# Moving 16 pieces of the adjacency mask from the first projection into the first attention, and sharing the last scaling between two engines

## The chip, the cores and the metric

The kernel runs on one core of a Trainium2 chip. A core has a matrix engine (TensorE, PE in the profile), a vector engine (VectorE, DVE), an activation engine (ScalarE, ACT), a general engine (GpSimd, POOL) and a queue engine (SyncE, SP). DMA engines move data between the large memory and the on-chip memory; SP, ACT and POOL start transfers. The metric is the device time of one execution in microseconds (us), lower is better.

## The reference, cut to what matters

Four graph layers run one after the other on 3327 nodes with 512 features. Each layer adds its output to its input and normalizes every row (subtract the mean, divide by the root of the variance plus 1e-5). All four use the same 3327 x 3327 integer matrix `adj`. Layers 0, 2 and 3 are graph attention; layer 1 averages up to 64 neighbours. The first layer's attention, cut:

```python
Wh = jnp.einsum('ni,hio->hno', h, W)                    # 8 heads of 64
f1 = jnp.einsum('hno,ho->hn', Wh, a1)
f2 = jnp.einsum('hno,ho->hn', Wh, a2)
e = jax.nn.leaky_relu(f1[:, :, None] + f2[:, None, :], 0.2)
masked = jnp.where(adj[None] > 0, e, NEG_INF)
attention = jax.nn.softmax(masked, axis=-1)
h_prime = jnp.einsum('hnm,hmo->hno', attention, Wh)
```

So every weight of the attention is multiplied by whether `adj` is positive. That mask is needed by all four layers, and it is made once.

## The kernel before, in words

**Tiles and halves.** The 3327 nodes are padded to 3328, which is NT = 26 tiles of 128 rows. The mask lies on chip as one tile `mask` of 128 x 26 x 3328 eight-bit numbers. The nodes that receive (the columns of the transposed matrix `adjT`) are cut into two halves of 1664, and each half into two quarters of 832.

**Making the mask.** A *piece* is one tile of 128 senders by one quarter: `mask_load` (L628) brings 128 x 832 integers of `adjT` into a buffer `raw`, and `mask_set` turns them into zeros and ones, on DVE by a comparison (L639) or on ACT by a steep sigmoid (L638). There are 104 pieces. The list `pieces` (L1103) holds first those of the quarters 0 and 1, tile by tile (52 pieces, the first half of the receivers), then those of quarter 2, then those of quarter 3. `mask_steps` makes a list of steps from them: step k loads piece k and sets piece k minus a lag. A load can start when its buffer is free, that is, when the piece that had it before has been set.

**The first projection (0 to about 142 us).** For each of the 26 tiles `project1` transposes a tile of x on PE (L266) and copies it (L267, ACT); `project2` multiplies it by the weights (16 matmuls L276 into two banks) and DVE empties the banks into `vt` (L282), which POOL's queue stores to memory (L288). One tile's `project2` runs after the next tile's `project1`. In the loop at L1138, after each tile's `project2`, three or four steps are taken alternately from `msteps`, the steps of the first EARLY = 5 x 26 / 2 + 3 = 68 pieces. They use eight buffers and a lag of five; ACT issues the first eight loads, SP the others; all are set by DVE. After tile 14, `prepare` and `cut` work on the columns of half 0, and at tile 20 the first row tiles `rb` are loaded for the attention. At the end `mean` (L298) multiplies a mean row.

**The first attention.** It runs through units (half, s): two halves and, in each, four slots of two heads, in the order (0,0), (0,1), (0,2), (0,3), (1,0) and so on. A unit loops over the 26 sender tiles j. For each j and head DVE makes `t` (L410, the larger of two terms times the mask of the half, 128 x 1664), ACT makes `y` from it (L413), PE multiplies `t` by the values `vj` (L433) and, two j later, `y` by small columns (L385). `t` has six buffers, `y` seven. Two lists are served once for each j: `background` (jobs in the code) and then `aside`. For this attention `aside` holds the steps of the 36 remaining pieces, with two buffers and a lag of one; the list of indices in L1175 says which of them ACT sets (k % 5 in 1, 3), DVE sets the others. They are kept in the program's order. `background` holds the jobs that `first_jobs` (L1155) gives for a unit, followed by those that the unit before left (ten steps of transposing its output and storing it), in this way: in (0,0) two empty jobs, the preparing and cutting for half 1 and eight jobs that count neighbours in half 0; in (0,1) the ten steps and then eight jobs `attend` (a weight load started by ACT, L1116, and eight matmuls, L1122); in (0,2) the ten steps and then eight jobs that count neighbours in half 1, from its mask (`count_jobs`, L669).

**The tail.** After the last layer's attention, `lasts` holds four groups of row tiles (4, 4, 4 and 1). For each group DVE finishes the sums and statistics, ACT takes the root (L1082), and `scale` for the group before it multiplies and shifts each of its tiles, on ACT (L1069) for every fourth tile and on DVE (L1071) for the others. Even tiles are stored by SP's queue, odd ones by POOL's (L133).

**What sets the order.** PE runs in the program's order. For the other engines a scheduler orders the instructions before the run, by its own estimates, unless `keep_in_program_order` pins one. An engine takes its instructions one after the other, so an instruction that waits holds those behind it, and the same holds for the transfers that one engine starts.

Of the kernel before, what the change touches and what calls it, by code (L numbers as in the profile page):

```python
# [32 lines left out]
def kernel(  # L33
# [12 lines left out]
    NT = (N + P - 1) // P  # L46
# [595 lines left out]
    def mask_steps(pool, pieces, lag, on_act, pinned, ahead=0):  # L642
        held = []

        def step(k):
            if k < len(pieces):
                held.append(mask_load(pool, *pieces[k], nc.scalar if k < ahead else nc.sync))
            if k >= lag:
                ins = mask_set(held[k - lag], *pieces[k - lag], on_act=(k - lag) in on_act)
                if pinned:  # L650
                    tc.keep_in_program_order(ins)
                held[k - lag] = None

        return [lambda k=k: step(k) for k in range(len(pieces) + lag)]
# [3 lines left out]
    def count_jobs(pool, half):  # L658
        jobs = []
        for s0, n in QUADS:  # L660
            i0, w_ = (half * HALF + s0) * P, n * P
            held = {}

            def counts(lo, hi, i0=i0, w_=w_, held=held):
                if lo == 0:
                    held["p"] = qp.tile([P, 4 * P], F32, name="pct", tag="q")
                for t in range(lo, hi):
                    g = t % 4
                    nc.tensor.matmul(held["p"][32 * g:32 * g + 32, :w_], onecol[:, 31 - t:63 - t],  # L669
                                     mask[:, t, i0:i0 + w_], start=t < 4, stop=t >= NT - 4)  # L670


            def none(i0=i0, w_=w_, held=held):
                ct = pool.tile([P, 4 * P], BF, name="ct", bufs=1)
                nc.scalar.copy(ct[:, :w_], held["p"][:, :w_])
                pn = qp.tile([P, 4 * P], F32, name="pn", tag="q")
                nc.tensor.matmul(pn[:, :w_], below, ct[:, :w_], start=True, stop=True)
                nc.vector.tensor_scalar(ct[:, :w_], pn[:, :w_], 128.0, None, op0=ALU.min)
                nc.sync.dma_start(out=ctd[:, i0:i0 + w_], in_=ct[:NT + 1, :w_])
                nb = pool.tile([P, 4 * P], F8, name="nb", bufs=1)  # L680
                nc.vector.tensor_scalar(nb[:, :w_], ct[:, :w_], 0.0, None, op0=ALU.is_equal, saturate=False)
                nc.sync.dma_start(out=mask[P - 1:P, NT - 1, i0:i0 + w_], in_=nb[NT:NT + 1, :w_])

            jobs += [lambda f=counts: f(0, NT), none]
        return jobs
# [216 lines left out]
    def third(first):  # L902
        with tc.tile_pool(name="col3", bufs=1) as cp, tc.tile_pool(name="at_r3", bufs=2, reuse_waits="tile") as rp:
# [3 lines left out]
            with tc.tile_pool(name="p_w", bufs=1, reuse_waits="tile") as wp, \  # L907
# [23 lines left out]
                for t0 in range(0, NT, 2):  # L931
# [4 lines left out]
                    for s, y in enumerate(ys):  # L936
                        t = t0 + s
# [22 lines left out]
            with tc.tile_pool(name="f3", bufs=2) as fp, tc.tile_pool(name="f4", bufs=1) as gp:  # L960
# [100 lines left out]
                def scale(q0, n):  # L1061
                    qs = slice(q0, q0 + n)
                    keep(nc.vector.reciprocal(rs[:, qs, 0], rs[:, qs, 0]))
                    keep(nc.vector.scalar_tensor_tensor(rs[:, qs, 1], mv[:, qs, 0], -1.0, rs[:, qs, 0],
                                                        op0=ALU.mult, op1=ALU.mult))
                    for q in range(q0, q0 + n):
                        y = g[:, q, :]
                        if q % 4 == 3:
                            keep(nc.scalar.activation(y, y, AF.Identity, bias=rs[:, q, 1:2], scale=rs[:, q, 0:1]))  # L1069
                        else:  # L1070
                            keep(nc.vector.tensor_scalar(y, y, rs[:, q, 0:1], rs[:, q, 1:2], op0=ALU.mult, op1=ALU.add))  # L1071
                        store(y, HALF + q, q)
# [14 lines left out]
    L0, L2, L3 = Layer(0, 8, False), Layer(2, 8, True), Layer(3, 4, True)  # L1087
# [3 lines left out]
    with tc.tile_pool(name="col0", bufs=1) as cp, tc.tile_pool(name="raw", bufs=2) as rawp, \  # L1091
            tc.tile_pool(name="at_r0", bufs=3, reuse_waits="tile") as rp:
        L0.columns(cp)
        L0.more_columns(cp)
        L0.piece_columns(cp)
        with tc.tile_pool(name="p_w", bufs=1, reuse_waits="tile") as wp, \
                tc.tile_pool(name="p", bufs=3, reuse_waits="tile") as pp, \
                tc.tile_pool(name="p_r", bufs=8, reuse_waits="tile") as rw0, \
                tc.tile_pool(name="p_ps", bufs=2, space=PSUM, reuse_waits="tile") as ps:
            if LAST < P:  # L1100
                nc.gpsimd.memset(mask[:, NT - 1, :], 0.0)
            nc.gpsimd.memset(mask[:, :, N:NP], 0.0)
            pieces = [(t, q) for t in range(NT) for q in range(2)] + [(t, q) for q in (2, 3) for t in range(NT)]  # L1103
            EARLY = 5 * NT // 2 + 3
            msteps = mask_steps(rw0, pieces[:EARLY], 5, (), False, 8)

            def load(t):
                xt = pp.tile([P, F], F32, name="xt", bufs=5)
                load_tile(xt, x, t, nc.sync if t < 3 else nc.gpsimd)
                return xt  # L1110


            def attend(pool, tag, dst, wT, a, k, held):
                H = a.shape[1] // 2
                wt = pool.tile([P, F], F32, name="wt", tag=tag, bufs=FC if tag == "wt" else 1)
                nc.scalar.dma_start(out=wt, in_=wT[k * P:(k + 1) * P, :])  # L1116
                if k == 0:
                    held["a"] = pool.tile([P, FC, 2 * H], F32, name=f"asb{H}", bufs=1)
                    nc.scalar.dma_start(out=held["a"], in_=a.rearrange("(c p) m -> p c m", p=P))
                    held["p"] = qp.tile([P, FC, 2 * H], F32, name="pa", tag="q")  # L1120
                for c in range(FC):
                    nc.tensor.matmul(held["p"][:, c, :], wt[:, c * P:(c + 1) * P], held["a"][:, k, :],  # L1122
                                     start=k == 0 and c == 0, stop=k == FC - 1,
                                     skip_group_check=True)
                if k == FC - 1:
                    nc.vector.tensor_copy(dst, held["p"] if len(dst.shape) == 3 else
                                          held["p"].rearrange("p c (e h) -> p c e h", e=2))

            def bank(e):
                return ps.tile([P, 512], F32, name=f"pw{e}")  # L1130

            xT = L0.project1(pp, ps, load(0), 0)
            held = {}
            wsb = wp.tile([P, FC, 2, FW + L0.H], F32, name="wsb")
            for k in range(FC):
                attend(pp, "wt", wsb[:, :, :, FW:], w0T, a0, k, held)
            load_wide(wsb, w0, nc.scalar)
            pend = (xT, 0)  # L1138
            for t in range(1, NT):
                xT = L0.project1(pp, ps, load(t), t)  # L1140
                L0.project2(pp, bank, wsb, *pend)
                pend = (xT, t)
                for _ in range(3 + t % 2):
                    if msteps:
                        msteps.pop(0)()
                if t == HALF + 1:
                    L0.prepare(pp, 0)
                    L0.cut(pp, 0)
                if t == NT - 6:
                    L0.first_rows = L0.rows(rp, 0, 0)  # L1150
            L0.project2(pp, bank, wsb, *pend)
            for f in msteps:
                f()
            L0.mean(pp, bank, wsb)

        def first_jobs(pool, half, s):

            if (half, s) == (0, 0):
                return [lambda: None] * 2 + [lambda: L0.prepare(f0, 1, "xr", 1, True), lambda: L0.cut(f0, 1, "h", 2, True)] + \
                    count_jobs(pool, 0)  # L1160
            if (half, s) == (0, 2):
                return count_jobs(pool, 1)
            if (half, s) == (0, 1):
                jobs = []
                for li, wT, a in ((2, w2T, a2), (3, w3T, a3)):
                    held = {}
                    jobs += [lambda k=k, li=li, wT=wT, a=a, held=held:
                             attend(f0, "xr", wa[li], wT, a, k, held) for k in range(FC)]
                return jobs
            return []  # L1170


        pieces = pieces[EARLY:]
        ends = []
        L0.attention(rp, first_jobs, mask_steps(rawp, pieces, 1, [k for k in range(len(pieces)) if k % 5 in (1, 3)], True),  # L1175
                     ending=lambda sp: ends.extend(finish(f0, x, L0, 0, 2, 2, nc.sync, None, sp)))

    with tc.tile_pool(name="col2", bufs=1) as cp:
# [60 lines left out]
```

## Time and profile before

| what | value |
|---|---|
| time, median of 3 runs | 3378.35 us (3377.11 to 3380.59) |
| the profiled execution | 3378.99 us, its span 3377.3 us |
| mean granted clock of PE | 0.986 |
| busy: PE, DVE, ACT, POOL | 3252.0, 2687.1, 2358.2, 239.6 us |
| first projection, 0 to 142.26 us: busy PE, DVE, ACT | 122.64, 85.34, 31.04 us |
| moved by DMA in that stretch | 344 GB/s on the average |
| tail, 3340 to 3377.3 us: busy DVE, ACT | 19.84, 13.98 us |

The profile is of one execution. Busy time is the time in which an engine worked; a granted clock of 1.00 is full speed. A row by stretch gives for each engine its busy microseconds and, in brackets, how many instructions began in it. A group's row names the line of the code, the engine, the operation, what it writes and reads, how often, its busy time and mean duration, and after the bar the idle time before it with what ended that time. "A <- B" in a list of waits means that A waited for B. The time of a whole execution is a little longer than its span from the first to the last instruction.

### The profile page before, as it was taken

The numbers are of one execution on the slowest core, as the hardware profiler recorded it, in microseconds if no ns is written. First come the engines' busy times: TensorE is split into PE (matmuls) and PEld (weight loads), VectorE is DVE, ScalarE is ACT, GpSimd is POOL, SyncE is SP. The second block draws the span as 40 slices with busy tenths as digits, with TensorE's granted clock in tenths as the row PEclk, the third lists the DMA queues.
The fourth block names the chain that finished last, engine by engine and source line by source line (L and its number), as shares of the span: only waits on it lengthen the run. The fifth ranks groups of instructions, "written<-read, shape, count | busy, mean of one in ns | idle before, by whom it ended". The sixth has DMA issues, their size and how long they took to land.

```text
span 3377.3 us, 47143 instructions
## 1 busy us (share of the span) xinstructions
PE 3252.0 (96%) x18424; PEld 1627.4 (48%) x18476; DVE 2687.1 (80%) x2619; ACT 2358.2 (70%) x2145; POOL 239.6 (7%) x389
## 2 busy tenths in 40 slices
PE   8799999999989999999989999999998999999997
PEld 7544344444444455545544444444446754455443
DVE  6799999999977544444449999999998766668887
ACT  2398998999953333333338999999997755558985
POOL 3100000000010111111110000000002000010110
PEclk9999999999999999999999999999998999999998
DMA  9544111110143433333320111111117411122311
GB/s 379 212 128 124 49 49 38 55 50 28 45 133 123 143 96 86 89 82 88 81 73 22 45 49 50 51 48 47 35 31 240 156 41 41 43 50 79 96 41 49
DMA packets 288014, 284.29 MB, mean 84 GB/s; under 512 B 107492, under 2 KB 223534, under 8 KB 287791
## 3 DMA queue, kind: packets, MB, share of 16 engines
q1 hardware_dynamic: 254063, 170.62, 16.7%
q0 software_dynamic: 28208, 102.96, 9.5%
q10 hardware_dynamic: 5520, 7.69, 0.7%
q8 instruction: 146, 2.39, 0.3%
q14 instruction: 77, 0.63, 0.1%
HBM read 212.01 MB, written 69.17 MB: 83 GB/s over the span
## 4 chain that ended last, share of the span: by engine, by line
PE 81%; DVE 5%; DMA 5%; issue 5%; ACT 4%; POOL 0%; SPq 0%; POOLq 0%; DVEq 0%; ACTq 0%
PE po L433 49%; PE acc L869 12%; PE pd L385 7%; PE pw L276 4%; DMA raw<-in_adjT_dram 3%; DVE t L410 3%; PE pz L737 3%; PE pi L740 2%; ACT y L413 1%; PE pk L829 1%; PE pt L461 1%; DMA h<-hd 1%; PE pa L1122 0%; DMA dd<-red 0%; PE pct L669 0%
## 5 line engine op out<-in xcount | busy, mean ns | idle before, releaser
L410 DVE SCALAR_TENSOR_TENSOR t<-rb,qc,mask 128x1664 f32<-128x1664 f32 x1040 | 1960.2, 1954 | 169.4 <-PE po L433 147.9
L413 ACT ACTIVATE y<-t,bi,sc 128x1664 fp8e4<-128x1664 f32 x1040 | 1770.5, 1768 | 309.5 <-PE pd L385 292.3
L433 PE MATMUL po<-t,vj 128*64 128x448 f32 (+3 forms) x8320 | 1908.6, 520 | 22.5 <-DVE t L410 19.8
L433 PEld LDWEIGHTS po<-t,vj 128*64 128x64 f32 (+1 forms) x8320 | 838.7, 148 | 970.4 <-issue 702.3
L869 PE MATMUL acc<-zs,kt 128*128 128x512 bf16 x1312 | 393.8, 381 | 2.2 <-issue 0.2
L276 PE MATMUL pw<-wsb,xT 128*128 128x264 f32 (+1 forms) x1248 | 300.2, 395 | 15.3 <-DVE vt L282 13.1
L869 PEld LDWEIGHTS <-kt 128*128 128x128 fp8e4 x2002 | 196.5, 98 | 242.1 <-issue 8.6
L821 ACT CAST pk<-cy 128x512 f32<-128x512 bf16 x169 | 99.1, 588 | 278.2 <-DVE kt L833 267.0
L385 PE MATMUL pd<-y,sden 128*32 128x448 fp8e4 (+1 forms) x4160 | 259.4, 341 | 10.4 <-ACT y L413 10.4
L276 PEld LDWEIGHTS pw<-wsb,xT 128*128 128x128 f32 x1248 | 239.8, 196 | 60.2 <-issue 10.6
L869 PE MATMUL acc<-zl,kt 128*128 128x512 bf16 x638 | 242.4, 380 | 0.6
L385 PEld LDWEIGHTS <-sden 128*32 128x32 bf16 x4160 | 117.5, 96 | 162.6 <-issue 139.8
L833 DVE SCALAR_TENSOR_TENSOR kt<-pk,mask 128x512 fp8e4<-128x512 f32 x169 | 116.1, 688 | 95.8 <-PE pk L829 95.8
L282 DVE TENSOR_TENSOR vt<-pw,dc 128x256 f32<-128x256 f32 x156 | 59.1, 418 | 147.4 <-ACT dc L277 142.7
L364 POOL DMA_DIRECT2D rb<-r x40 | 21.4, 534 | 1668.2 <-DVE t L410 1653.8
L280 ACT COPY rc<-pw 128x8 f32<-128x8 f32 (+1 forms) x78 | 12.7, 163 | 155.6 <-PE pw L276 155.6
L737 PE MATMUL pz<-wn,xT 128*128 128x512 f32 x208 | 95.8, 604 | 1.6 <-ACT xT L731 1.6
L841 DVE SCALAR_TENSOR_TENSOR y<-acc,cnt,bnb 128x512 f32<-128x512 f32 x26 | 19.5, 750 | 96.9 <-PE acc L869 89.5
L705 POOL DMA_DIRECT2D cy<-ctd x91 | 68.1, 748 | 385.5 <-ACT pk L821 312.8
L740 PE MATMUL pi<-wl,xT 128*128 128x512 f32 x208 | 93.5, 592 | 0.0
L639 DVE TENSOR_SCALAR mask<-raw 128x832 fp8e4<-128x832 int32 (+2 forms) x90 | 54.7, 615 | 39.7 <-DMA raw<-in_adjT_dram 39.2
L154 ACT ACT_TABLE_LOAD x46 | 59.0, 1283 | 37.3 <-DVE mv L153 36.7
(187 smaller groups left out, 1704.7 us busy)
## 6 DMA issues: line engine op xcount, KB each, us to landing
vj<-v SPq DMA_DIRECT2D x312, 128.0 KB
rb<-r POOLq DMA_DIRECT2D x40, 832.0 KB, 4.6
raw<-in_adjT_dram SPq DMA_DIRECT2D x67, 416.0 KB
cy<-ctd POOLq DMA_DIRECT2D x78, 256.0 KB, 4.0
h<-hd SPq DMA_DIRECT2D x61, 256.0 KB
v<-vt SPq DMA_DIRECT2D x50, 256.0 KB
hd<-hb SPq DMA_DIRECT2D x48, 256.0 KB
xr<-x POOLq DMA_DIRECT2D x45, 256.0 KB, 3.1
```

The lines of the kernel that those rows point to most:

```text
L276: nc.tensor.matmul(pw[e][:, :FW + H], xT[:, c, :], wsb[:, c, e, :], start=c == 0, stop=c == FC - 1)
L282: nc.vector.tensor_tensor(vt[:, hs, :], pw[e][:, :FW].rearrange("p (h d) -> p h d", d=D), self.dc[:, t, hs].rearrange("p (h e) -> p h e", e=1)
L385: nc.tensor.matmul(pd[c][32 * kk:32 * kk + 32, :w_], lhsT, rhs, start=(kk, c) not in seen, skip_group_check=final is not None, stop=last a ...
L410: nc.vector.scalar_tensor_tensor(t, rb[k], self.qc[:, j, h:h + 1], mask[:, j, i0:i0 + IW], op0=ALU.max, op1=ALU.mult)
L413: nc.scalar.activation(y, t, AF.Sigmoid, bias=self.bi[:, j, h:h + 1], scale=self.sc[:, j, h:h + 1], saturate=False)
L433: nc.tensor.matmul(po[c][k * D:(k + 1) * D, :z - a_], vj[:, j % 2, k * D:(k + 1) * D], ts[k][:, a_:z], start=j == 0, stop=j == NT - 1)
L705: nc.gpsimd.dma_start(out=cy[:, :n, :], in_=ctd[t:t + n, b * GW:(b + 1) * GW] .rearrange("(o t) i -> o t i", o=1).to_broadcast([P, n, GW]))
L737: nc.tensor.matmul(pz, xT[:, c, :], wn[:, c, :], start=c == 0, stop=c == FC - 1)
L740: nc.tensor.matmul(pi, xT[:, c, :], wl[:, c, :], start=c == 0, stop=c == FC - 1)
L821: nc.scalar.copy(pks[k % 2], carry[b, t // 4 * 4][:, t % 4:t % 4 + 2, :])
L833: nc.vector.scalar_tensor_tensor(kt, pk, NEIGHBOURS, mask[:, t:t + 2, i0:i0 + GW], op0=ALU.is_le, op1=ALU.mult, saturate=False)
L869: nc.tensor.matmul(acc, kts[t][:, s * P:(s + 1) * P], zs(t, c) if c < 2 else zl[:, t, :], start=t == 0 and c == 0, stop=t == NT - 1 and c ...
```

## The change

EARLY becomes 52, so in the projection only the pieces of quarters 0 and 1 are made, and two or three steps are taken after a tile instead of three or four. The other 52 pieces (36 before) are made in the attention. There ACT sets those whose index modulo 9 is 1, 3, 5 or 7, DVE the others. With the lag of one that is 53 steps, one for each j, so they fill the units (0,0) and (0,1), and one step remains for the first j of unit (0,2). In unit (0,2) four empty jobs stand ahead of the counting of half 1. In the tail ACT scales every second row tile instead of every fourth.

```diff
@@ scale(q0, n)
-                        if q % 4 == 3:
+                        if q % 2 == 1:
                             keep(nc.scalar.activation(y, y, AF.Identity, bias=rs[:, q, 1:2], scale=rs[:, q, 0:1]))
                         else:
                             keep(nc.vector.tensor_scalar(y, y, rs[:, q, 0:1], rs[:, q, 1:2], op0=ALU.mult, op1=ALU.add))
@@ first projection
-            EARLY = 5 * NT // 2 + 3
+            EARLY = 2 * NT
             msteps = mask_steps(rw0, pieces[:EARLY], 5, (), False, 8)
...
-                for _ in range(3 + t % 2):
+                for _ in range(2 + (t % 3 == 1)):
                     if msteps:
                         msteps.pop(0)()
@@ first_jobs
             if (half, s) == (0, 2):
-                return count_jobs(pool, 1)
+                return [lambda: None] * 4 + count_jobs(pool, 1)
@@ first attention
         pieces = pieces[EARLY:]
         ends = []
-        L0.attention(rp, first_jobs, mask_steps(rawp, pieces, 1, [k for k in range(len(pieces)) if k % 5 in (1, 3)], True),
+        L0.attention(rp, first_jobs, mask_steps(rawp, pieces, 1, [k for k in range(len(pieces)) if k % 9 in (1, 3, 5, 7)], True),
                      ending=lambda sp: ends.extend(finish(f0, x, L0, 0, 2, 2, nc.sync, None, sp)))
```

## The prediction

> **What bounds the kernel now.** I read the page first, then the stretches, waits and timelines of the three places that the change touches: the first projection (0 to 142 us), the first attention's first units (142 to 460 us) and the tail (from 3344 us). The page's slices and chain name three suspects:
>
> ```profile
> DMA  9544111110143433333320111111117411122311
> PE po L433 49%; PE acc L869 12%; PE pd L385 7%; PE pw L276 4%; DMA raw<-in_adjT_dram 3%; DVE t L410 3%; PE pz L737 3%; PE pi L740 2%; ACT y L413 1%; PE pk L829 1%; PE pt L461 1%; DMA h<-hd 1%; PE pa L1122 0%; DMA dd<-red 0%; PE pct L669 0%
> L639 DVE TENSOR_SCALAR mask<-raw 128x832 fp8e4<-128x832 int32 (+2 forms) x90 | 54.7, 615 | 39.7 <-DMA raw<-in_adjT_dram 39.2
> ```
>
> The DMA engines are full only in the first slice and a half; mask pieces hold 3% of the chain, some 100 us, and DVE idled 39 us for them. The busy times by stretch, with columns PE, PEld, DVE, ACT, POOL, granted clock, DMA share and GB/s, say where:
>
> ```profile
> 30.00:40.00 10.00, 10.00 (x52) 8.57 (x51) 7.82 (x17) 2.36 (x11) 2.53 (x4) 1.00 1.03 379
> 110.00:120.00 10.00, 6.95 (x34) 5.75 (x34) 4.23 (x8) 1.02 (x5) 2.21 (x4) 1.00 1.03 380
> 130.00:140.00 10.00, 10.00 (x49) 8.60 (x48) 3.41 (x10) 2.70 (x12) 1.08 (x2) 1.00 0.26 95
> ...
> 142.26:255.95 113.69, 101.85 (x745) 43.79 (x747) 112.16 (x96) 98.17 (x70) 0.70 (x2) 0.94 0.39 111
> 255.95:359.17 103.22, 102.84 (x761) 48.91 (x759) 101.28 (x63) 92.13 (x64) 0.95 (x2) 1.00 0.35 105
> 359.17:460.07 100.90, 99.42 (x801) 40.24 (x799) 100.25 (x62) 93.92 (x66) 1.06 (x2) 1.00 0.14 46
> ```
>
> In the projection the DMA is at 380 to 413 GB/s until 125 us, while PE has holes (6.95 of 10). Once the masks are in, at 130 us, PE is full and DMA nearly empty. The last three rows are the attention's units (0,0), (0,1), (0,2), cut where I count every 52nd L410: DVE is 98 to 99% busy. The unit without extra work, (0,3), takes 96.9 us, which is 52 L410 at 1.863. So in the attention DVE time is end time. The waits of the projection (0 to 145 us: total, times, longest) show how a late piece reaches PE:
>
> ```profile
> DVE mask L639 <- DMA raw<-in_adjT_dram: 38.5, 37, 2.8
> PE pw L276 <- DVE vt L282: 12.4, 9, 3.0
> ```
>
> and the timelines of DVE and, below it, PE (start, duration, engine, line, in brackets the idle time before it) show one such case:
>
> ```profile
> 112.61 0.59 DVE L639 TENSOR_SCALAR mask<-raw 128x832 fp8e4<-128x832 int32 x1 [1.02 <-DMA raw<-in_adjT_dram]
> 115.50 0.59 DVE L639 TENSOR_SCALAR mask<-raw 128x832 fp8e4<-128x832 int32 x1 [2.30 <-DMA raw<-in_adjT_dram]
> 116.01 0.75 DVE L282 TENSOR_TENSOR vt<-pw,dc 128x256 f32<-128x256 f32 x2
> ...
> 116.57 3.80 PE L276 MATMUL pw<-wsb,xT 128*128 128x264 f32 x16 [3.05 <-DVE vt L282]
> ```
>
> DVE waits for a piece, `vt` stands behind it, and PE waits for `vt` to empty its bank.
>
> **What the Trainium skill says.** "TensorE: Matmul & The Clock Gate", Architectural detail: ScalarE and VectorE queues are strict FIFO; the four timeline lines above agree. "DMA: Bandwidth & Descriptors", Issuing engines are not separate DMA queues: loads started by SP, ACT and POOL share 16 engines. The trace agrees: all three issue here and the sum stays at 380 to 413 GB/s. So fewer mask bytes free the others. "ScalarE: Activation LUTs", What ACT_TABLE_LOAD costs: an ACTIVATE with a pointer bias takes 280 ns + 0.833 ns an element and back to back overlaps by 93 ns; for 832 that is an estimate of 973 and 880. The trace has 982, and 0.88 between starts (228.65 to 229.53).
>
> **Projection: 16 pieces fewer.** A piece is 128 x 832 x 4 B = 0.426 MB. Per tile of 128 rows before: 3.5 pieces (1.49 MB), x (0.262) and the v store (0.262), 2.02 MB, at 400 GB/s 5.0 us. PE needs 4.00 us a tile where nothing holds it (its transposes start at 31.57, 35.58, 39.58, 43.58). Groups 2 and 22 start at 18.66 and 116.57, 4.9 us each: the DMA sets the pace. After: 2.33 pieces, 1.52 MB, 3.8 us, just under PE. A piece still has 8 buffers and is set 5 steps after its step, so about 8/2.33 x 4.0 = 13.7 us pass from a free buffer to its use, which tolerates jitter.
>
> PE alone would run group 2 at 18.66, group 25 at 18.66 + 23 x 4.00 = 110.7, and with the last two groups (7.29) end at 118.0. It ended at 138.6, 20.6 later: 12.4 waiting for `vt` (of it 1.96 at 91.48, behind the preparing and cutting of half 0's columns), 1.16 for an x tile at 27.5, 2.8 for the preparation's transposes at 78 to 81, 1.75 in a group at lowered clock, 2.5 of small gaps. The part that late bytes cause is 12.4 - 1.96 + 1.16 = 11.6. Left over I expect 1.6: from 93 to 110 three row loads (`rb`, 0.852 MB each, 2.56 MB, 6.4 us at 400) compete, and the slack of 0.2 us a tile and the waiting time of 13.7 us cover most of it. So -10, bounds -5 (half the waits stay) and -13 (the one behind the cut goes as well: fewer sets, DVE has more room). The 59 steps offered in tiles 1 to 25 suffice for 52 + 5, so nothing is left to run after the loop. The eight loads that ACT issues spread over tiles 1 to 4, and SP's loads move forward with their buffers; the attention's first `vj` loads wait behind fewer of SP's raw loads (12.3 us there now). The start of the attention moves with PE's end, since L410's first waits for L298.
>
> **Attention: 36 pieces become 52.** By the index rules DVE sets 22 and then 29, ACT 14 and then 23. By unit, DVE goes 15 to 14, 7 to 14, 0 to 1, ACT 10 to 11, 4 to 12. A set on DVE adds 0.50 (150.32 to 150.82), on a bound engine: 7 x 0.50 = +3.5. Around it: DVE's idle of 0.79 at 338 to 341, where PE lags, is filled (-0.8; PE needs 3.0 + 1.0 + 0.5 us a step in the eight steps with weight products L1122, against DVE's 3.73 now and 4.0 after). Sets wait for their piece twice now, 0.77 in all, one a step with two buffers; 16 more, +0.4. ACT in unit (0,1): 92.1 + 8 x 0.88 = 99.2 busy of some 106, hidden behind DVE; it idles 9.5 us from 296 to 375 for y buffers that PE frees, so most fits there; +0.4. Behind a late set on DVE stand its L410s, then PE and ACT. SP gets 16 more loads in order with `vj`, at 0.33 each over 100 us, hidden: `vj` has four buffers of two steps. If that cover went, a `vj` late by a step would cost PE 3.5. The counts of half 1 start four steps later in unit (0,2), 22 jobs for 26 steps: same work on PE, 0, with 1.0 either way. In sum +3.5, bounds +1.5 and +6.
>
> **Tail.** Three times in the last stage DVE hands a scaling to ACT:
>
> ```profile
> 3369.62 1.46 DVE L1071 TENSOR_SCALAR g<-g,rs 128x512 f32<-128x512 f32 x3
> 3370.99 0.16 DVE L1063 RECIPROCAL rs<-rs 128x1 f32<-128x1 f32 x1
> ...
> 3369.61 0.81 ACT L1069 ACTIVATE g<-g,rs 128x512 f32<-128x512 f32 x1
> ```
>
> One is worth 1.37/3 = 0.46 on DVE; ACT's two take about 1.5 from the quad's start, before the next root is due. DVE ends 1.37 earlier. But nine tiles' stores (2.36 MB) fill the DMA from 3368.2 to 3375.3 at 330 GB/s, and their first moves by one scaling only: -0.5, bounds -0.2 and -1.2. Odd rows all go to POOL's queue as before.
>
> **Sum.** -10 + 3.5 - 0.5 = -7.0. The profiled execution took 3378.99 (span 3377.3, 1.7 around it), so 3372.0 with a span of 3370.3; the median of the runs is 3378.35, 0.64 lower, so 3371.3. A measurement of this kernel can tell about 0.2%, 6.8 us: the forecast lies at that edge.
>
> **Rivals.** (1) The projection still runs at the DMA's pace. For: 3.8 against 4.0 is a thin margin, and the rate was 318 to 360 in three stretches before 100 us; at 360 a tile needs 4.2. Against: those stretches also had stalls that throttled demand. -5 + 3.5 - 0.5: 3376.3. (2) More goes than I count: -13, +2.7 as PE's slack eats more, -1: 3367. (3) Slower: ACT becomes the bound in unit (0,1). It issues the eight `wt` loads of L1116 in order between its activations, into one buffer, and a load takes 2.94 from issue to PE's product. If ACT falls behind PE there, PE, in its fixed order, waits up to 8 x 2.94 = 23.5, less some 4 of room before DVE runs out of t buffers: 3391. It decides from 11/8, about 1.4 us a load. For: ACT goes to 94% of the unit. Against: in that stretch ACT waits for PE, not PE for ACT (PE waited 1.3 for `wt` in all), and PE at 4.5 a step is slower than ACT at 3.7. (4) Nothing to measure because the scheduler sets pieces in another order than written: now 73 steps at 3.5 a tile end at tile 21 as written, which speaks against it.
>
> **How the numbers follow.** Forecast 0.52, with its own range 3368.3 to 3374.3 (faster 0.29, same 0.23); rival 1 0.19, same; rival 2 0.18, faster; rival 3 0.09, slower; rival 4 0.02, same. So faster 0.47, same 0.44, slower 0.09. The range 3366.0 to 3377.5 takes in the forecast, nearly all of rival 1 and most of rival 2, and leaves out rival 3.
>
> **What would show it.** Right: PE's L298 starts near 128.6, not 138.6; PE's waits for `vt` before 145 us fall from 12.4 to about 3.5; DVE's waits for raw there to under 15; GB/s in the projection below 390 in most stretches; unit (0,1) takes near 106 us with DVE over 98%, (0,0) 113; the last L1071 ends 1.4 earlier relative to its stage, the DMA's end 0.5. Wrong: L298 later than 133 with the DMA still full, unit (0,1) over 109, or PE waiting for `wt` by more than 1 us each.

## The result and the profile after

The changed kernel takes 3373.53 us (median of 17 runs, 3370.45 to 3379.43) against 3378.58 for the kernel before (17 runs), a ratio of 0.9986 with a 95% interval of 0.9979 to 0.9992. That is 5.05 us by the medians, 4.7 by the ratio: faster, by less than 0.2%. The forecast was 3371.3, its range 3366.0 to 3377.5. The prediction thought that about 0.2% (6.8 us) could be told; the interval of 17 runs a side ends below 1, so the direction is clear, and the gain is small. The profiled execution has a span of 3372.7 us, before 3377.3.

The slices and the chain on the page of the changed kernel:

```profile
DMA  9455211110144433333220111111117411122211
PE po L433 49%; PE acc L869 12%; PE pd L385 7%; PE pw L276 5%; DVE t L410 4%; PE pz L737 3%; PE pi L740 2%; DMA raw<-in_adjT_dram 2%; ACT y L413 1%; PE pk L829 1%; PE pt L461 1%; DMA h<-hd 0%; DMA dd<-red 0%; DVE xr L196 0%; PE pa L1122 0%
L639 DVE TENSOR_SCALAR mask<-raw 128x832 fp8e4<-128x832 int32 (+3 forms) x81 | 49.4, 618 | 26.1 <-DMA raw<-in_adjT_dram 25.9
```

The mask's share of the chain fell from 3% to 2%, `t` on DVE rose from 3% to 4%. The DMA's load moved from the second slice into the third, fourth and fifth. The same exchange, by stretches (PE, PEld, DVE, ACT, POOL, granted clock, DMA share, GB/s), and below it the two waits of the projection that the forecast named:

```profile
60.00:70.00 10.00, 9.04 (x45) 7.37 (x45) 6.08 (x13) 2.23 (x11) 2.42 (x4) 1.00 1.03 403
110.00:120.00 10.00, 10.00 (x53) 8.59 (x52) 3.50 (x8) 2.75 (x12) 1.08 (x2) 1.00 0.21 81
...
134.19:246.57 112.38, 101.50 (x745) 43.14 (x747) 111.34 (x96) 98.96 (x71) 0.70 (x2) 0.95 0.39 110
246.57:355.45 108.88, 105.33 (x769) 48.55 (x767) 104.92 (x70) 98.16 (x71) 1.07 (x3) 0.98 0.54 158
355.45:458.31 102.86, 100.27 (x793) 40.98 (x791) 100.75 (x62) 94.36 (x67) 0.93 (x2) 0.98 0.16 50
```

```profile
DVE mask L639 <- DMA raw<-in_adjT_dram: 24.5, 26, 2.6
...
PE pw L276 <- DVE vt L282: 3.6, 5, 1.8
```

Three things stand out. The projection's DMA is still full from 50 to 80 us, and then empties at 110 us where it was full before: the saving came all at once, late. Unit (0,1) grew from 103.2 to 108.9 us, more than the forecast's 106. And the granted clock, 1.00 in the units (0,1) and (0,2) before, is 0.98 in both.

| stretch | before | after | difference | forecast |
|---|---|---|---|---|
| start of L298 (PE has projected all tiles) | 138.38 | 130.32 | -8.1 | -10 |
| unit (0,0) | 113.69 | 112.37 | -1.3 | about -0.5 |
| unit (0,1) | 103.17 | 108.88 | +5.7 | about +3 |
| unit (0,2) | 100.91 | 102.86 | +1.95 | about +0.5 |
| last L410 of the first layer | 945.28 | 942.51 | -2.8 so far | |
| from there to the first L410 of the next attention | 807.8 | 805.4 | -2.3 | 0 |
| from there to the last L410 of all | 1584.4 | 1585.5 | +1.2 | 0 |
| last L410 to the end | 39.85 | 39.19 | -0.66 | -0.5 |

The -2.3 and the +1.2 are not the change's: the twelve profiled kernels of this study, which don't differ in those two stretches, take 804.8 to 811.0 us and 1582.7 to 1587.2 us there. Without them the profile shows about -8.1 + 5.3 - 0.7 = -3.5 us, inside the interval of the timed runs.

### The profile page after: what moved, and what is told of

It is laid out like the page before. It is cut to its first block, busy times and chain, and to the rows that moved or that the text cites. A ratio compares the mean times of both kernels' runs of the same rounds, so it can differ in the third digit from the quotient of the medians.

```text
span 3372.7 us, 47193 instructions
## 1 busy us (share of the span) xinstructions
PE 3253.1 (96%) x18476; PEld 1625.2 (48%) x18476; DVE 2680.2 (79%) x2607; ACT 2367.1 (70%) x2157; POOL 238.6 (7%) x389
## 4 chain that ended last, share of the span: by engine, by line
PE 81%; DVE 6%; issue 4%; DMA 4%; ACT 3%; POOL 0%; SPq 0%; ACTq 0%; POOLq 0%; DVEq 0%
PE po L433 49%; PE acc L869 12%; PE pd L385 7%; PE pw L276 5%; DVE t L410 4%; PE pz L737 3%; PE pi L740 2%; DMA raw<-in_adjT_dram 2%; ACT y L413 1%; PE pk L829 1%; PE pt L461 1%; DMA h<-hd 0%; DMA dd<-red 0%; DVE xr L196 0%; PE pa L1122 0%
## 5 line engine op out<-in xcount | busy, mean ns | idle before, releaser
L410 DVE SCALAR_TENSOR_TENSOR t<-rb,qc,mask 128x1664 f32<-128x1664 f32 x1040 | 1960.9, 1953 | 171.4 <-PE po L433 150.3
L869 PE MATMUL acc<-zs,kt 128*128 128x512 bf16 x1352 | 401.2, 380 | 0.0
L639 DVE TENSOR_SCALAR mask<-raw 128x832 fp8e4<-128x832 int32 (+3 forms) x81 | 49.4, 618 | 26.1 <-DMA raw<-in_adjT_dram 25.9
```

The source lines that it names most:

```text
L410: nc.vector.scalar_tensor_tensor(t, rb[k], self.qc[:, j, h:h + 1], mask[:, j, i0:i0 + IW], op0=ALU.max, op1=ALU.mult)
L869: nc.tensor.matmul(acc, kts[t][:, s * P:(s + 1) * P], zs(t, c) if c < 2 else zl[:, t, :], start=t == 0 and c == 0, stop=t == NT - 1 and c ...
```

## The experiments

**Where the scheduler put the sets.** The order in which DVE ran its instructions in the profiles shows how many sets stand ahead of the second half of each tile's `vt` (counted from the half of the tile before), from the first tile to the last:

```
before         3 3 4 3 3 3 3 4 3 3 3 3 4 2 5 1 1 4 3 3 4 3 0 0 0 0
after          3 3 4 3 3 3 3 4 3 3 3 3 4 0 6 2 1 1 0 0 0 0 0 0 0 0
pinned         0 0 0 2 3 2 2 3 2 2 3 2 2 3 2 2 3 2 2 3 2 2 3 2 2 1
before_pinned  0 0 2 4 3 4 3 4 3 4 3 4 3 4 3 4 2 2 4 3 3 3 3 0 0 0
```

In the changed kernel the scheduler ignored the loop's new pace of 2.33 a tile. It kept 3 to 4 for the first 13 tiles, and the pieces ran out with the 18th. (The last two lists are of experiments below.) So the forecast's "3.8 us a tile, just under PE" never came about: the matmuls of the 20th tile start at 103.5 us before and at 103.4 in the changed kernel, and the gain is in the six tiles after it, at most 4.0 us apart in the changed kernel and up to 7.3 before. To test that, the sets were kept in the program's order:

```diff
-            msteps = mask_steps(rw0, pieces[:EARLY], 5, (), False, 8)
+            msteps = mask_steps(rw0, pieces[:EARLY], 5, (), True, 8)
```

> The changed kernel with the projection's sets kept in the program's order, so DVE's list has 2.33 of them a tile instead of 3 to 4 until they run out at tile 18. Theory: the scheduler's own pace kept the DMA full until 95 us and cost PE the waits that remained, so now L298 starts at 126 to 128 (130.3 in the changed kernel), PE's waits for vt are under 2 us, GB/s stays below 390 in most stretches, and the time falls by 2.5 to 4 us. Rival: the remaining waits are PE's and ACT's own (copies of xT, preparation): L298 stays within 1 us of 130.3. Other rival: pinned sets hold vt up, L298 after 132.

Measured: 3365.38 us, ratio to the kernel before 0.9959 (0.9944 to 0.9974), and L298 at 120.39 instead of 130.32. That is more than the theory's own numbers. Stretches, PE's timeline and a wait of the pinned kernel:

```profile
40.00:50.00 10.00, 10.00 (x51) 8.57 (x50) 7.25 (x16) 2.41 (x9) 4.27 (x6) 1.00 1.02 378
60.00:70.00 10.00, 10.00 (x51) 8.57 (x50) 6.75 (x17) 2.76 (x11) 4.21 (x6) 1.00 1.02 401
110.00:120.00 10.00, 10.00 (x49) 8.55 (x48) 6.29 (x14) 1.66 (x8) 1.82 (x4) 1.00 0.81 251
```

```profile
43.21 0.60 PE L266 MATMUL pt<-ident,xt 128*128 128x128 f32 x4
43.65 3.73 PE L276 MATMUL pw<-wsb,xT 128*128 128x264 f32 x16
47.21 0.60 PE L266 MATMUL pt<-ident,xt 128*128 128x128 f32 x4
47.65 3.73 PE L276 MATMUL pw<-wsb,xT 128*128 128x264 f32 x16
```

```profile
DVE mask L639 <- DMA raw<-in_adjT_dram: 1.4, 3, 0.6
```

PE takes a tile every 4.00 us without a gap here; its one longer step after 30 us is 5.9 us, at the preparation. DVE waits 1.4 us for pieces where it waited 38.5 before and 24.5 in the changed kernel. The DMA is hardly slower in two of these stretches (378 and 401 GB/s), but almost nobody waits for it: the pieces land before DVE asks for them. The changed kernel, in contrast, still has this at the same place (PE's timeline):

```profile
46.72 3.80 PE L276 MATMUL pw<-wsb,xT 128*128 128x264 f32 x16 [1.80 <-DVE vt L282]
```

Is it the order alone? The kernel before, with only its 68 sets pinned in the same way:

```diff
-            msteps = mask_steps(rw0, pieces[:EARLY], 5, (), False, 8)
+            msteps = mask_steps(rw0, pieces[:EARLY], 5, (), True, 8)
```

> The kernel before with its 68 sets kept in the program's order (3.5 a tile). It tells whether order alone made the gain of the pinned run, or order together with fewer bytes. Theory (both): at 3.5 pieces a tile needs 2.02 MB, 5.0 us at 400 GB/s, so the DMA still sets the pace whatever the order: L298 at 132 to 139 (before 138.4, pinned 120.4), DMA at 380 to 410 GB/s until 120 us, time at most 6 us below before. Rival (order alone): L298 near 122, time 15 us below before or better, since the attention then has no more than before.

Measured: 3377.3 us, ratio 0.9998 (0.9989 to 1.0006), L298 at 140.04. One stretch of it:

```profile
60.00:70.00 10.00, 8.02 (x31) 6.35 (x30) 6.37 (x14) 1.13 (x5) 1.88 (x4) 0.83 1.03 408
```

The order alone gives nothing in the timed runs. (The profile is of the slowest of the 12, 3384.02 us, so its L298 may lie later than usual.) With 3.5 pieces a tile the DMA is full at 408 GB/s and PE waits; with 2.33 and the order it isn't the bound any more. Fewer bytes a tile was the right idea, but it takes both.

**The projection's gain alone.** The kernel before without the 16 pieces:

```diff
-            msteps = mask_steps(rw0, pieces[:EARLY], 5, (), False, 8)
+            msteps = mask_steps(rw0, pieces[:2 * NT], 5, (), False, 8)
-                for _ in range(3 + t % 2):
+                if t <= 16:
+                    nc.gpsimd.memset(mask[:, t - 1, IW:IW + IW // 2], 0.0)
+                for _ in range(2 + (t % 3 == 1)):
```

> The kernel before, but the 16 pieces that the change moves are never loaded or set (zeros stand in their place, written by POOL in 16 small fills), so part of the mask and the results that need it are left out; the attention still makes its 36. It prices the projection's gain alone. If the gain is what the changed kernel shows: L298 starts near 130.3 (before 138.4), units (0,0), (0,1), (0,2) stay at 113.7, 103.2, 100.9, the time is about 8 us below before. If the forecast's size was right and something else in the changed kernel held the projection: L298 at 128.5, 10 us below. If the gain came from elsewhere: L298 unchanged within 2 us.

Measured: 3369.26 us, ratio 0.9975 (0.9966 to 0.9983), 9.5 us below before by the medians. L298 at 131.81, units 112.95, 102.54, 100.90. The projection's gain stands without the attention's cost. Its size is not clean: POOL, which also starts the loads of x, was busy with the fills, and PE worked only 5.43 of the 10 us from 20 to 30; the three units came out 1.4 us shorter than before.

**The attention's cost alone.** The kernel before, with 52 pieces in the attention though the projection makes 68:

```diff
-        pieces = pieces[EARLY:]
+        pieces = pieces[2 * NT:]
-        L0.attention(rp, first_jobs, mask_steps(rawp, pieces, 1, [k for k in range(len(pieces)) if k % 5 in (1, 3)], True),
+        L0.attention(rp, first_jobs, mask_steps(rawp, pieces, 1, [k for k in range(len(pieces)) if k % 9 in (1, 3, 5, 7)], True),
-                return count_jobs(pool, 1)
+                return [lambda: None] * 4 + count_jobs(pool, 1)
```

> The kernel before with the changed attention alone: the projection makes its 68 pieces, and the attention makes 52, the 16 a second time, with the changed split between the engines and the later counts. It prices the attention's cost alone. By the changed kernel's trace: L298 near 138.4, units 112.4, 108.9, 102.9, that is 5 to 6.5 us slower than before. By the forecast (seven sets of 0.50 on DVE, little else): 3.5 slower, unit (0,1) at 106.

Measured: 3381.67 us, ratio 1.0007 (0.9998 to 1.0016), 3.0 us above before by the medians. Units 113.45, 107.05, 102.72, together 5.45 more than before; L298 came 1.1 us earlier. The cost by this trace is nearer to the changed kernel's (6.3 over the three units) than to the forecast's 3.5; the timed runs can't tell the two apart. Unit (0,1) had its full clock here, unit (0,2) 0.98; what that is worth comes next.

**Why unit (0,1) is dearer.** In the changed kernel PE stood once for a weight, and ACT had started that load late. PE's and ACT's timelines:

```profile
295.32 3.21 PE L433 MATMUL po<-t,vj 128*64 128x448 f32 x16
...
301.84 1.07 PE L1122 MATMUL pa<-asb,wt 128*128 128x16 f32 x8 [2.44 <-DMA wt<-in_w2T_dram]
302.84 4.71 PE L433 MATMUL po<-t,vj 128*64 128x448 f32 x16
```

```profile
294.24 5.10 ACT L413 ACTIVATE y<-t,bi,sc 128x1664 fp8e4<-128x1664 f32 x3
299.07 0.35 ACTq L1116 DMA_DIRECT2D wt<-in_w2T_dram  x1
```

The buffer was free at 295.3, when the product before had ended. DVE then idled 1.9 us for PE in this unit. It is the mechanism of the forecast's slower rival, once instead of eight times.

The wait had a second price. Right behind it a group of 16 matmuls took 4.71 us where the group ahead of it took 3.21, for the granted clock fell to half in that stretch (columns as above):

```profile
303.21:306.62 3.41, 3.41 (x12) 1.22 (x10) 3.41 (x3) 3.41 (x3) 0.00 (x0) 0.50 0.50 93
```

Unit (0,2) has such a stretch too, from 364.65 to 368.06, behind waits of PE at the start of the unit. Between 20 and 470 us the twelve profiles show 37 falls to half clock, and in the 3.4 us ahead of each of them PE was busy for at most 1.61. The profiles in which the attention is the changed one, with the products in (0,1) and their loads started by ACT, sort by it; the first row is the kernel before:

| profile | unit (0,1), granted clock | unit (0,2), granted clock |
|---|---|---|
| before | 103.17, 1.00 | 100.91, 1.00 |
| changed | 108.88, 0.98 | 102.86, 0.98 |
| old_tail (below) | 109.00, 0.98 | 102.91, 0.98 |
| no_delay (below) | 106.95, 1.00 | 103.19, 0.98 |
| twice16 | 107.05, 1.00 | 102.72, 0.98 |
| pinned | 108.89, 0.98 | 101.31, 1.00 |

In all five of the changed attention PE waits once for a late weight in (0,1), 2.2 to 2.5 us, and in three of them a stretch at half clock follows. Without that stretch the unit takes 107.0 us, one more than the forecast's 106; with it 108.9. In (0,2) the stretch goes with 1.4 to 1.9 us. So an estimate of the attention's cost at full clock is twice16's 5.45 with pinned's 101.31 in place of its 102.72: about 4.0, near the forecast's 3.5. This is a sorting of profiles; no run changed the clock alone. Why a stretch follows one such wait and not another stays open.

The first trial took ACT out of the weight loads:

```diff
-                nc.scalar.dma_start(out=wt, in_=wT[k * P:(k + 1) * P, :])
+                (nc.scalar if tag == "wt" else nc.sync).dma_start(out=wt, in_=wT[k * P:(k + 1) * P, :])
```

> The changed kernel with the eight weight loads of the attention (L1116) started by SP instead of ACT. Theory: unit (0,1) costs 108.9 instead of the forecast's 106 since ACT, fuller with sets, started one of these loads late and PE stood 2.4 to 2.9 us for it: now PE's waits for wt fall from 6 to under 2 us, unit (0,1) takes 106 to 106.5, the time falls by 2 to 3 us. Rival: the added work on DVE and PE alone makes 108.9, or SP's order holds the loads up as long: unit (0,1) stays above 108.

Measured: 3374.85 us, ratio to before 0.9991 (0.9985 to 0.9998); unit (0,1) 109.7 at full clock, 2.7 more than the 107.0 above. The theory failed as put. PE waited less for weights, and a new wait took the place, on DVE (waits from 230 to 360 us):

```profile
DVE wa L1126 <- PE pa L1122: 4.4, 2, 3.0
...
PEld pa L1122 <- DMA wt<-in_w2T_dram: 1.1, 1, 1.1
...
PEld pa L1122 <- DMA wt<-in_w3T_dram: 0.6, 1, 0.6
PE pa L1122 <- DMA wt<-in_w2T_dram: 0.4, 1, 0.4
```

The copies of the finished products (L1126) stood in DVE's list ahead of L410s, and DVE waited there 4.4 us for PE. So the second trial took the products out of the unit altogether, on top of the pinned kernel:

```diff
-            if (half, s) == (0, 1):
+            if (half, s) in ((0, 3), (1, 1)):
                 jobs = []
-                for li, wT, a in ((2, w2T, a2), (3, w3T, a3)):
+                for li, wT, a in ((2, w2T, a2),) if half == 0 else ((3, w3T, a3),):
```

> The pinned kernel with the eight weight products of unit (0,1) moved, four to unit (0,3), four to (1,1). Theory: unit (0,1) takes 108.9 because PE, ACT and DVE are all near full there and the products make PE late; without them it is bound by DVE: 96.9 + 14 x 0.505 + under 1.5 = 104.5 to 105.5, and (0,3) and (1,1) take 97 to 98.5 (96.9 now): 1.5 to 4 us faster than pinned, about 3362. Rival (the fuller ACT alone makes it late, without the products too): (0,1) stays above 107.5.

Measured: 3360.97 us, ratio 0.9946 (0.9933 to 0.9960). Unit (0,1) took 105.68, a little over the theory's 104.5 to 105.5, (0,3) 96.99 and (1,1) 98.15. The row of the unit:

```profile
236.41:342.09 105.68, 100.96 (x705) 44.62 (x703) 104.06 (x68) 99.37 (x72) 1.08 (x3) 1.00 0.50 146
```

The unit takes 3.2 us less than in the pinned kernel and the two others together 1.4 more. Without the products this profile shows no late weight, no wait of DVE for PE and a full clock in the unit. About 1.9 of the 3.2 is that clock: against the 107.0 of the profiles with the products and a full clock, the unit gains 1.3, no more than the other two lose. ACT has more than ever to do here (99.37) and isn't in the way. By the median this is the fastest kernel of the study, some 17 us below the kernel before and 12 below the changed one; its interval overlaps that of the pinned kernel.

Is DVE the bound, at 0.50 a set? Two runs moved six sets from ACT to DVE, one with the products in (0,1), one without:

```diff
-        L0.attention(rp, first_jobs, mask_steps(rawp, pieces, 1, [k for k in range(len(pieces)) if k % 9 in (1, 3, 5, 7)], True),
+        L0.attention(rp, first_jobs, mask_steps(rawp, pieces, 1, [k for k in range(len(pieces)) if k % 3 == 1], True),
```

> The pinned kernel with ACT setting every third piece, 17 instead of 23, DVE 35 instead of 29. Theory of DVE as the bound: units (0,0) and (0,1) together cost six sets more, +3.0 us (221.2 to 224.2). Rival (ACT is too full and holds up the weight loads and the emptying of PE's banks): (0,1) falls below 108.9 and the boundary to (0,2) loses its stalls, (0,0) + (0,1) + (0,2) at or below pinned's 322.5.

> The kernel of pin_spread with ACT setting every third piece (17, not 23), DVE 35 instead of 29. With the weight products gone from unit (0,1), DVE should be the bound of (0,0) and (0,1), so that each set moved to DVE shows its price. Theory: six sets at 0.50, +3.0 us: (0,0) + (0,1) from 218.0 to 220.5 to 221.5, time 2 to 3 us above pin_spread. Rival (ACT still late without the products): at or below 218.5.

Measured: with the products 3366.60 us, ratio 0.9962 (0.9948 to 0.9975), units 113.11, 107.99, 100.49, 321.6 together against 322.5 in the pinned kernel, where 3.0 more was the theory. The comparison isn't clean: the pinned kernel has a stretch at half clock in (0,1), and this one has none. With 1.9 us taken off the pinned kernel for it, an estimate from the table, the six sets cost about 1.0; whether the emptier ACT (286.2 busy in these three units against 291.3) paid for the rest isn't shown. Without the products 3364.36, ratio 0.9957 (0.9941 to 0.9974), (0,0) and (0,1) 221.67 against 218.02, +3.65, and over the three units +2.9: near the theory's 3.0. In this pair both profiles have a full clock in (0,1) and (0,2). The price of a set on DVE is about right where DVE alone is the bound.

**The empty jobs.** The changed kernel without them:

```diff
-                return [lambda: None] * 4 + count_jobs(pool, 1)
+                return count_jobs(pool, 1)
```

> The changed kernel without the four empty jobs ahead of the counts of half 1 in unit (0,2). Forecast: same work on PE, unit (0,2) 102.9 as in the changed kernel, within 1.0, all others unchanged. If the counts fall on the stalls of the unit's start and add to them, (0,2) is 104 or more.

Measured, one execution: 3371.17 us, unit (0,2) 103.19 against 102.86. Nothing, as forecast. Unit (0,1) took 106.95 here, though nothing in it had changed: five profiles with its products in place and the same split (this, the changed kernel, pinned, twice16, old_tail) span 106.95 to 109.00, in the order of their clock as shown above. So the excess over the forecast's 106 is 1 us, and 3 with a stretch at half clock.

**The tail.** The changed kernel with the old tail:

```diff
-                        if q % 2 == 1:
+                        if q % 4 == 3:
```

> The changed kernel with the old tail (ACT scales every fourth tile). Forecast for the tail: the time from the last L410 to the end is 39.2 in the changed kernel and 0.5 longer here, 39.7 (39.85 in the kernel before); DVE's last L1071 ends 1.37 later. If sharing gives nothing since the stores fill the DMA: 39.2 to 39.4, with DVE's end later all the same.

Measured, one execution: 3374.71 us; from the last L410 to the end 39.40 us, 0.21 longer than in the changed kernel. DVE's last scalings in the old tail and in the changed one:

```profile
3348.07 0.24 DVE L578 RECIPROCAL rec<-rec 128x13 f32<-128x13 f32 x1
3367.04 0.55 DVE L1071 TENSOR_SCALAR g<-g,rs 128x512 f32<-128x512 f32 x1
```

```profile
3347.95 0.24 DVE L578 RECIPROCAL rec<-rec 128x13 f32<-128x13 f32 x1
3365.55 0.57 DVE L1071 TENSOR_SCALAR g<-g,rs 128x512 f32<-128x512 f32 x1
```

From the reciprocal L578 to the end of the last scaling it is 19.52 against 18.18: DVE ends 1.34 earlier, as forecast, and 0.2 of it reaches the end. That 0.2 is within the scatter: the five profiles with the old tail take 39.23 to 39.99 us from the last L410 to the end, the seven with the new one 39.08 to 39.56, 0.3 less on the average. The stores fill the DMA either way (342 GB/s from 3365 to 3370 us here, 332 in the changed kernel).

## Why the prediction was right or wrong

**The time and the direction: right, in part by luck.** 3373.53 lies in the range and in the forecast's own range; the gain was put 2.2 us too large. The number alone doesn't tell the forecast (3371.3) from rival 1 (3376.3): it lies between them. And the projection's share came near its forecast by another way than the one worked out.

**Projection: right in sign, -8.1 for -10, and the working of it wrong.** The step that failed is "After: 2.33 pieces, 1.52 MB, 3.8 us, just under PE". The loop doesn't set that pace; the scheduler does, and it left 3 to 4 sets a tile for the first 13 tiles. The waits for `vt` did fall as put, from 12.4 to 3.6 (forecast 3.5), but 2.1 of waiting for ACT's copy of `xT` was new. DVE's wait for pieces fell to 24.5 where under 15 was forecast, and the DMA stayed above 400 GB/s from 50 to 80 us. (Nor was it at 380 to 413 GB/s all the way to 125 us in the kernel before: it moved 358 from 40 to 50, 318 from 90 to 100 and 260 from 120 to 130.) The forecast named the possibility, in rival 4, and set it aside because the old loop's 73 steps end at tile 21 as written. That agreement was chance: in the old list, too, the sets begin with the first tile and stand at the scheduler's pace, not at the loop's. Where the step's premise is made true, by pinning, PE does run at 4.00 us a tile and the projection gains 18 us, more than the forecast's bound of 13: I had counted the preparation, a group at lowered clock and the small gaps as staying, and most of them went. The group at lowered clock was itself a price of late pieces, for it stood right behind a wait for `vt`; in the kernel before:

```profile
55.98 5.49 PE L276 MATMUL pw<-wsb,xT 128*128 128x264 f32 x16 [1.93 <-DVE vt L282]
```

**Attention: +5.3 for +3.5, and near it at full clock.** 0.50 for a set on DVE is about right (spread_third: 3.65 for six). What the sum left out is what PE's waits bring: one late weight load in (0,1), about 1 us over the forecast's 106, where "ACT ... most fits there; +0.4" had put little, and the two stretches at half clock, about 1.9 in (0,1) and 1.4 to 1.9 in (0,2), for which it put nothing. In (0,2) PE waited 0.9 for banks that ACT emptied late (`ob`); the pinned kernel has that wait too (1.1), with a full clock, and takes 101.31, so the wait alone is worth little. "DVE's idle of 0.79 is filled" was the wrong way round: DVE's idle for PE in (0,1) rose to 1.9 (1.2 in no_delay and twice16), and DVE was busy for 96% of the unit, not over 98%.

**Tail: -0.2 by the direct comparison for -0.5**, at the forecast's bound of -0.2 and within the scatter; DVE's part was right (1.34 for 1.37).

**The rivals.** The first, a projection still at the DMA's pace, held for its first two thirds. The third, late weight loads, was real and small, one load instead of eight, but dearer than its own length where half clock followed. None turned the sign.

## What to carry to other kernels

A count in a loop sets a pace only if something holds the scheduler to it: read the order in which the engine ran, not the loop, before a rate is put against a bandwidth. Moving bytes off a full transfer queue paid in full here only when demand a tile fell below supply *and* the consumer's instructions stood no earlier than the data came; either one alone gave nothing (order) or less than half (bytes). When work is moved into a stage whose engines are all above 90%, price it on each of them, and ask whether PE will have to wait: here a wait of 2.44 us for a weight was followed by 3.41 us at half clock, and so it went in three of the six profiles with such a late weight. Before a difference of one or two microseconds between two profiles is put down to a cause, compare the granted clock of that stretch in both.
